# A Perceiver kernel on one core: the second block's convolution, running means and perceptron in four parts with a list of turns, its routing behind the second and the fourth part

## The chip, the cores and the metric

The kernel runs on one core of a Trainium2 chip. The core has a matrix engine (TensorE, "PE" in the profile, with its weight loads as "PEld"), VectorE (DVE), ScalarE (ACT), GpSimd (POOL), and a queue that issues transfers (SyncE, SP). Each works through its own instructions in a fixed order and waits for the others through semaphores. The metric is the time of one execution on the device in microseconds (us), smaller is better. All data is float32; in the trace one matrix product of this type is two records of PE, each with its weight load, and a transpose is one.

## The reference, cut to what matters

The network has four blocks, each of cross-attention, a sequence layer and a feed-forward layer, over x of 16 sequences by 64 steps by 256 features. The change touches the sequence layer and the routing of the second block (L1):

```python
x = x + L1_xattn(layernorm(x), ctx, ...)
x = x + L1_attn(layernorm(x), ...)
x = x + L1_ffn(layernorm(x), ...)

def L1_attn(x, ...):
    h = ln(x, ln_conv_g, ln_conv_b)
    x = x + causal_conv(h, conv_w, width=4, groups=4) + conv_b
    h = ln(x, ln_attn_g, ln_attn_b)
    q, k, v = h @ Wq.T + bq, h @ Wk.T + bk, h @ Wv.T + bv
    pooled_q = cumsum(q, axis=1) / arange(1, S + 1)
    pooled_k = cumsum(pooled_q * k, axis=1) / arange(1, S + 1)
    x = x + pooled_k * v
    h = ln(x, ln_boom_g, ln_boom_b)
    return x + gelu(h @ Wb.T + bb) @ Wu.T + bu

def L1_ffn(x, ...):
    probs = softmax(x @ router_W + router_b)
    top1 = argmax(probs)
    gates = one_hot(top1, 8) * probs
    h = relu(x @ W1[e] + b1[e])
    y = h @ W2[e] + b2[e]
    return sum over experts e of gates[e] * y
```

Wb makes 1024 features of 256, Wu 256 of 1024; the experts have 256, 1024 and 256.

## The kernel before

The 1024 rows of x (16 sequences of 64 steps) stay in on-chip memory as eight tiles of 128 rows, `xs`. The layers run one after the other (`run`, the `plan` table); each opens its own pools of on-chip memory and of the eight PSUM banks. Weights come through a ring of two slots: `pack()` waits for a layer's loads, which were issued earlier, and starts the next ones as soon as a slot is free.

`L1_attn` works through the layer in stages, each over all 1024 rows. `norm_x` (L184) normalizes the eight tiles, two transposes each. `norm` with `put_padded` does it again, with the affine part on VectorE (L1487), into `hp`, in which each sequence has three zero columns ahead. The convolution is products of 512 columns over shifted views of `hp`; ScalarE adds the bias (L1502). `add_by_features` transposes the outcome back and adds it (L1514). A third norm writes `hT` (L1521). Then, in four pieces (halves of the rows, halves of the features), q, k and v are products of 512 columns; `running_mean` is a sum along the steps on VectorE (L1540) and a product (L1541), k and v enter from PSUM (L1555, L1557). A second `add_by_features`, a fourth norm, and the perceptron, in two halves of 512 rows: eight products up with Gelu on ScalarE (L1572), then for each of four tiles eight products down, one of the bias row, and the addition to x (L89).

A norm of a tile (`norm_tile`, L150 to L161) is statistics on VectorE (L154, L156, L158), a power on POOL (L160), and a subtraction and product on VectorE (L170).

`L1_ffn` begins with `norm_x`, sends the rows to device memory (`keep_row`, L1082), makes the logits of eight tiles, and `route` (L1084 to L1143) finds each row's expert, its place among that expert's rows, and a table from place to row. `blocks` (L1237 to L1285) counts how many blocks of 128 rows each expert needs and lists the weight rows and token rows of each block. Then b2, weighted with the gate, is added to x for each tile: a transpose of the gates (L1360), a copy, a product, an addition. A block gathers its weights (`wa`, `wb`) and its rows (`hb`) by POOL's indirect transfers (L1304), transposes the rows (L179), and makes its products `ph` and `po`; 14 blocks run here.

Inside `L1_attn` and `L1_ffn` the order of instructions on each engine comes from a scheduler, which goes by priorities and a cost table when the kernel is built. Where `manual_schedule` names an engine, that engine keeps the order of the program text, as TensorE does in the cross-attention before.

## Time and profile before

| | |
|---|---|
| median of three runs | 3025.43 us (3025.0 to 3040.91) |
| the profiled execution | 3029.32 us, span of its instructions 3027.5 us |
| granted TensorE clock, mean | 0.942 |
| PE, PEld | 2704.1 us (89%), 1955.0 us (65%) |
| DVE, ACT, POOL | 1482.0 us (49%), 1022.6 us (34%), 309.4 us (10%) |
| transfers | 253.55 MB, mean 84 GB/s |

Busy time is the sum of an engine's instructions; a busy PE need not be PE at its peak, since ends of products are modelled and the clock changes. The granted clock is a share of full speed. In the timeline each line has a start, a duration, the engine, the line of the program, the operation, "output<-inputs", the shape and a count; what ended the idle time before it stands in brackets. The chain that ended last is followed back from the last instruction through what released each step. Many matrix products have the line of the helper `mm` (L69), so they are told apart by the names of their tiles.

### The profile page before, as it was taken

What the parts mean: (1) busy time and instruction counts of PE and PEld (TensorE: products, weight loads), DVE (VectorE), ACT (ScalarE), POOL (GpSimd) and SP (SyncE); (2) the same over time, 40 slices, a digit from 0 to 9 for tenths busy, and PEclk for the clock granted to TensorE, in tenths of its full rate; (3) what the DMA queues carried; (4) which work ended last, traced back from release to release, by engine and by line L of the source; (5) the groups of instructions that cost most, each with busy time, mean ns of one, the idle gap of its engine ahead of it and who ended that gap; (6) DMA issues with size and microseconds to landing.
All of it is one profiled execution on the core that took longest, in us unless ns stands there. A gap on an engine that the chain in (4) does not pass through costs nothing.

```text
span 3027.5 us, 42618 instructions
## 1 busy us (share of the span) xinstructions
PE 2704.1 (89%) x16840; PEld 1955.0 (65%) x16840; DVE 1482.0 (49%) x3177; ACT 1022.6 (34%) x2290; POOL 309.4 (10%) x428
## 2 busy tenths in 40 slices
PE   7888997999999787979999997887998898887899
PEld 3566784666666346857777776874766666665668
DVE  3654115666666643234444344223445657658581
ACT  2331122555555111223333321122335455455330
POOL 1112223000000112310101011201001000000000
PEclk9997997999999897989999998998999999998999
DMA  9504771101010004811111113450212212121110
GB/s 242 171 27 159 253 230 51 36 26 36 26 36 22 28 9 171 281 49 54 55 44 47 60 42 116 163 217 22 67 43 84 74 51 83 56 67 53 57 36 7
DMA packets 79220, 253.55 MB, mean 84 GB/s; under 512 B 15151, under 2 KB 26954, under 8 KB 69290
## 3 DMA queue, kind: packets, MB, share of 16 engines
q1 hardware_dynamic: 59562, 165.01, 17.5%
q0 software_dynamic: 13312, 80.28, 7.8%
q10 hardware_dynamic: 6144, 5.51, 0.5%
q8 instruction: 134, 2.20, 0.3%
q14 instruction: 68, 0.56, 0.1%
HBM read 233.80 MB, written 14.82 MB: 82 GB/s over the span
## 4 chain that ended last, share of the span: by engine, by line
PE 64%; DVE 11%; ACT 4%; DMA 3%; issue 3%; POOL 1%; SPq 1%; ACTq 0%; DVEq 0%; POOLq 0%
PE misc L69 11%; PE sc L500 8%; PE halves L69 7%; PE gu L69 5%; PE misc L235 4%; PE ps_h L69 4%; PE po L69 4%; PE ps_t L235 3%; PE sc L69 2%; PE misc L864 2%; ACT p L225 2%; PE o L915 2%; PE misc L878 2%; DMA back<-ys,route_at 2%; DVE x L1926 2%
## 5 line engine op out<-in xcount | busy, mean ns | idle before, releaser
L223 DVE TENSOR_REDUCE nmx<-sc 128x1 f32<-128x1024 f32 x264 | 311.6, 1218 | 234.9 <-PE sc L500 150.4
L225 ACT ACTIVATE p<-sc,nmx 128x1024 f32<-128x1024 f32 x264 | 294.6, 1116 | 312.1 <-DVE nmx L223 311.4
L500 PE MATMUL sc<-ctxT,qp 128*128 128x512 f32 (+1 forms) x1024 | 353.4, 599 | 0.0
L500 PEld LDWEIGHTS sc<-ctxT,qp 128*128 128x128 f32 (+1 forms) x1024 | 137.8, 189 | 153.0 <-issue 151.6
L69 PE MATMUL halves<-ctx,pT 128*128 128x192 f32 x1024 | 191.0, 343 | 9.4 <-DVE xs L89 4.0
L69 PEld LDWEIGHTS halves<-ctx,pT 128*128 128x128 f32 x1024 | 178.4, 203 | 12.3 <-DVE xs L89 4.5
L160 POOL TENSOR_TENSOR ln_rs<-ln_ve,nhalf 128x1 f32<-128x1 f32 x120 | 67.0, 563 | 1142.3 <-DVE ln_ve L158 1081.6
L69 PE MATMUL misc<-ctx,pT 128*128 128x192 f32 x1024 | 177.6, 327 | 0.5 <-DVE qT L465 0.5
L69 PEld LDWEIGHTS misc<-ctx,pT 128*128 128x128 f32 x1024 | 166.3, 191 | 2.1 <-DVE qT L465 1.0
L235 PE MATMUL ps_t<-ident,p 128*128 128x128 f32 x1088 | 147.2, 277 | 21.9 <-ACT p L225 14.0
L1916 ACT ACTIVATE da<-rep,al 128x252 f32<-128x252 f32 x256 | 114.7, 498 | 115.0 <-DVE x L1926 95.6
L1926 DVE TENSOR_TENSOR_SCAN x<-da,x 128x512 f32<-128x512 f32 x128 | 151.9, 1210 | 1.9 <-ACT da L1916 1.4
L235 PE MATMUL misc<-ident,p 128*128 128x128 f32 x1024 | 139.8, 283 | 14.1 <-ACT p L225 6.7
L237 ACT COPY pT<-ps_t 128x512 f32<-128x512 f32 x182 | 104.3, 585 | 139.3 <-PE ps_t L235 137.3
L235 PEld LDWEIGHTS ps_t<-ident,p 128*128 128x128 f32 x1088 | 127.1, 143 | 36.0 <-ACT p L225 17.7
L235 PEld LDWEIGHTS misc<-ident,p 128*128 128x128 f32 x1024 | 112.2, 143 | 40.2 <-ACT p L225 13.3
L69 PE MATMUL ps_h<-r,w 128*128 128x256 f32 x512 | 115.3, 385 | 0.0
L237 ACT COPY pT<-misc 128x512 f32<-128x512 f32 x128 | 75.0, 586 | 114.9 <-PE misc L235 114.6
L69 PEld LDWEIGHTS ps_h<-r,w 128*128 128x128 f32 x512 | 97.8, 192 | 16.6 <-issue 2.9
L69 PE MATMUL gu<-dT,wa 128*128 128x128 f32 (+1 forms) x864 | 104.7, 280 | 3.7 <-ACT dT L64 2.4
L239 DVE COPY pT<-misc 128x512 f32<-128x512 f32 x128 | 88.2, 689 | 39.4 <-PE misc L235 28.9
L69 PE MATMUL po<-wb,hid 128*128 128x256 f32 (+1 forms) x440 | 105.9, 388 | 0.2 <-ACT hid L1380 0.2
(468 smaller groups left out, 4449.5 us busy)
## 6 DMA issues: line engine op xcount, KB each, us to landing
ctx<-in_ctx SPq DMA_DIRECT2D x48, 768.0 KB
ctxT<-in_ctxT SPq DMA_DIRECT2D x48, 512.0 KB
w<-in_L2f_W SPq DMA_DIRECT2D x24, 1024.0 KB
rep<-dus SPq DMA_DIRECT2D x256, 64.0 KB
ctxT<-in_ctxT SPq DMA_DIRECT2D x16, 768.0 KB
ctxT<-in_ctxT SPq DMA_DIRECT2D x96, 128.0 KB
ys<-yb ACTq DMA_DIRECT2D x40, 128.0 KB
bc_rep<-bcs SPq DMA_DIRECT2D x32, 128.0 KB
```

What stands on the lines that cost most here:

```text
L69: self.nc.tensor.matmul(out, lhsT, rhs, start=n == 0, stop=n == len(pairs) - 1)
L160: nc.gpsimd.tensor_tensor(rs, ve, self.nhalf, ALU.pow)
L223: self.nc.vector.tensor_reduce(nmx, sc, AX.X, ALU.max, negate=True)
L225: self.nc.scalar.activation(p, sc, AF.Exp, bias=nmx, accum_out=sums)
L235: self.nc.tensor.transpose(ps[:, u, :], p[:, at : at + 128], self.ident)
L237: self.nc.scalar.copy(pT[:, 4 * g : 4 * g + 4, :], ps)
L239: self.nc.vector.tensor_copy(pT[:, 0:4, :], ps)
L500: nc.tensor.matmul(sc[u][:, bass.ts(kh, 512)], qp[n][par][rows, h : h + 2, :].rearrange("p h q -> p (h q)"), ctx[0][rows, at], start=n == ...
L864: nc.tensor.matmul(ps[kh], wk[:, kh, cols], cT[:, bass.ts(kh, 512)], start=True, stop=False)
L878: nc.tensor.matmul(ps[kh][:, u, :], cT[:, 512 * kh + at : 512 * kh + at + 128], wv[:, 0, :], start=u == 0, stop=False,)
L1916: nc.scalar.activation(da[:, g, :, 1:], now[j][:, 0, :].rearrange("p (b s) -> p b s", s=S)[:, :, 1:], AF.Exp, scale=al[:, col : col + 1],)
L1926: nc.vector.tensor_tensor_scan(flat, da.rearrange("p g b s -> p (g b s)"), flat, 0.0, ALU.mult, ALU.add)
```

## The change

`L1_attn` is written anew as a generator `part(p)` for 256 rows (two tiles), which yields at 15 places, and a generator `routing(first)` for four tiles, with five. `turns` lists which generator goes on next: 0, 1, 3, 4 are the four parts, 2 and 5 the routing of the first and of the last four tiles. TensorE keeps this order; the other engines are ordered by the scheduler as before.

Within a part, two tiles are normalized together, with one power for both; the affine part of the norms moves to ScalarE, as do the biases of k and v; four transposes share one PSUM bank; products have 256 columns; both halves of the features go through one sum of 512 columns. The layer closes its other PSUM pool and has eight one-bank buffers. The perceptron's outcome is normalized, sent to device memory and transposed by the part itself. `routing` holds the logits, `route`, and the addition of b2, all for four tiles; `L1_ffn` is left with `blocks` and the blocks. The router's weights and b2 are loaded with the perceptron's, so there is one pack less; the loads of the next block are started behind the turns.

```diff
     def gate(self, name, n=NT):
-        return (self.sb or self.lp).tile([128, n, E], F32, name=name)
+        return (self.sb or self.lp).tile([128, n, E], F32, bufs=self.gate_bufs, name=name)
...
-    def keep_row(self, i):
-
-        self.nc.sync.dma_start(self.hs[1 + i * 128 : 1 + (i + 1) * 128], self.htok[:, i, :])
+    def keep_row(self, i, x=None):
+
+        self.nc.sync.dma_start(self.hs[1 + i * 128 : 1 + (i + 1) * 128], self.htok[:, i, :] if x is None else x)
...
-    def pack_L1_gate(self):
-        self.slot()
-        w, row = self.load("L1f_rW"), self.load_row("L1f_rb")
-        b2 = self.carve(E, D)
-        self.nc.sync.dma_start(b2, self.a["L1f_b2"])
-        return w, row, b2
-
...
     def L1_ffn(self):
         nc = self.nc
-        rw, rb, b2 = self.pack()
-        self.norm_x()
-        self.routed = r = self.route_setup(1)
-        for i in range(NT):
-            self.keep_row(i)
-        gates = self.gate("gates")
-        for _ in self.route(r, self.gate_logits(rw, rb), 0, gates):
-            pass
-        self.rows, self.tokens = self.blocks(r, L1_BLOCKS)
-        for i in range(NT):
-            pg = self.misc([E, 128])
-            nc.tensor.transpose(pg, gates[:, i, :], self.ident)
-            gT = self.lp.tile([E, 128], F32, tag="gT", bufs=2, name="gT")
-            self.evict(gT, pg)
-            po = self.misc([128, D])
-            self.mm(po, [(gT, b2)])
-            self.add_to_x(i, po)
+        self.rows, self.tokens = self.blocks(self.routed, L1_BLOCKS)
+
         def block(j, own=""):
...
     def pack_L1_boom(self):
         self.slot()
-        return self.load("L1a_WbT"), self.load("L1a_WuT"), self.load_row("L1a_bu")
+        boom = self.load("L1a_WbT"), self.load("L1a_WuT"), self.load_row("L1a_bu")
+        gate = self.load("L1f_rW"), self.load_row("L1f_rb")
+        b2 = self.carve(E, D)
+        self.nc.sync.dma_start(b2, self.a["L1f_b2"])
+        return boom, gate, b2
 
     def L1_attn(self):
...
+        (cv, *qkv), ((wb, wu, bu), (rw, rb), b2) = self.pack(), self.pack(ahead=False)
+        self.lps_close()
+        routed, self.gate_bufs = self.route_setup(1), 4
+        later = self.later_steps()
+        def tokens(p, name):
+            return self.lp.tile([128, 2, D], F32, name=f"{name}{p}")
+        def features(p, name):
+            return self.lp.tile([128, 2, CHUNK], F32, name=f"{name}{p}")
+        def normalized(x, out):
+            mv = self.small.tile([128, 2, 2], F32, name="ln_mv2")
+            for t in range(2):
+                st = self.small.tile([128, 6], F32, name="ln_st")
+                nc.vector.bn_stats(st, x[:, t, :])
+                nc.vector.bn_aggr(mv[:, t, :], st)
+            rs = self.small.tile([128, 2], F32, name="ln_rs2")
+            nc.vector.tensor_scalar(rs, mv[:, :, 1], 1e-5, None, ALU.add)
+            nc.gpsimd.tensor_tensor(rs, rs, self.nhalf.to_broadcast([128, 2]), ALU.pow)
+            for t in range(2):
+                nc.vector.tensor_scalar(
+                    out[:, t, :], x[:, t, :], mv[:, t, 0:1], rs[:, t : t + 1], ALU.subtract, ALU.mult
+                )
+        def transposed(x):
+            ps = self.misc([128, 2, CHUNK])
+            for t in range(2):
+                for c in range(2):
+                    nc.tensor.transpose(ps[:, c, bass.ts(t, 128)], x[:, t, c * 128 : (c + 1) * 128], self.ident)
+            return ps
+        def affine(x, to, g, b):
+            ps = transposed(x)
+            for c in range(2):
+                src = ps[:, c, :]
+                if len(to.shape) == 4:
+                    src = src.rearrange("p (b s) -> p b s", s=S)
+                nc.scalar.activation(
+                    to[:, c], src, AF.Identity, bias=self.col(b, c), scale=self.col(g, c)
+                )
+        def added(x, to):
+            ps = self.misc([128, 2, D])
+            for t in range(2):
+                for c in range(2):
+                    nc.tensor.transpose(ps[:, t, bass.ts(c, 128)], x[:, c, t * 128 : (t + 1) * 128], self.ident)
+            nc.vector.tensor_tensor(to, to, ps, ALU.add)
+        by_features = [None] * NC
+        def part(p):
+            x = self.xs[:, 2 * p : 2 * p + 2, :]
+            hp = self.lp.tile([128, 2, 4, S + 3], F32, name=f"hp{p}")
+            nc.gpsimd.memset(hp[:, :, :, 0:3], 0.0)
+            x1, w = tokens(p, "x1"), tokens(p, "lnw")
+            normalized(x, x1)
+            normalized(x1, w)
+            yield
+            affine(w, hp[:, :, :, 3:], "L1a_lcg", "L1a_lcb")
+            yield
+            ps = self.misc([128, 2, CHUNK])
+            conv = features(p, "hTs")
+            for c in range(2):
+                self.mm(
+                    ps[:, c, :].rearrange("p (b s) -> p b s", s=S),
+                    [(cv[:, c, k, :], hp[:, c, :, k : k + S]) for k in range(4)],
+                )
+            for c in range(2):
+                nc.scalar.activation(conv[:, c, :], ps[:, c, :], AF.Identity, bias=self.col("L1a_conv_b", c))
+            yield
+            added(conv, x1)
+            w = tokens(p, "lnw")
+            normalized(x1, w)
+            yield
+            hT = features(p, "hTs")
+            affine(w, hT, "L1a_lag", "L1a_lab")
+            yield
+            got = []
+            for m, name in zip(qkv, "qkv"):
+                ps = self.misc([128, 2, CHUNK])
+                got.append(features(p, name))
+                for o in range(2):
+                    self.mm(ps[:, o, :], [(m[:, c, o * 128 : (o + 1) * 128], hT[:, c, :]) for c in range(2)])
+                for o in range(2):
+                    nc.scalar.activation(
+                        got[-1][:, o, :], ps[:, o, :], AF.Identity, bias=self.col(f"L1a_b{name}", o)
+                    )
+                if name == "q":
+                    yield
+            q, k, v = got
+            inv = self.inv_s.unsqueeze(1).to_broadcast([128, 8, S])
+            for y in (k, v):
+                flat = q.rearrange("p c t -> p (c t)")
+                nc.vector.tensor_tensor_scan(flat, later, flat, 0.0, ALU.mult, ALU.add)
+                steps = q.rearrange("p c (b s) -> p (c b) s", s=S)
+                nc.vector.tensor_tensor(steps, steps, inv, ALU.mult)
+                nc.vector.tensor_tensor(q, q, y, ALU.mult)
+            yield
+            added(q, x1)
+            w = tokens(p, "lnw")
+            normalized(x1, w)
+            nc.gpsimd.tensor_tensor(x, x, x1, ALU.add)
+            yield
+            hT = features(p, "hTs")
+            affine(w, hT, "L1a_lbg", "L1a_lbb")
+            yield
+            if p < 2:
+                g = self.act.tile([128, 8, CHUNK], F32, tag=("htok", "hT")[p], name="hid")
+            else:
+                g = self.lp.tile([128, 8, CHUNK], F32, name=f"hid{p}")
+            for m2 in range(4):
+                ps = self.misc([128, 2, CHUNK])
+                for u in range(2):
+                    m = 2 * m2 + u
+                    self.mm(ps[:, u, :], [(wb[:, c, m * 128 : (m + 1) * 128], hT[:, c, :]) for c in range(2)])
+                for u in range(2):
+                    m = 2 * m2 + u
+                    nc.scalar.activation(g[:, m, :], ps[:, u, :], AF.Gelu, bias=self.col("L1a_bb", m))
+                if m2 % 2:
+                    yield
+            for t in range(2):
+                po = self.misc([128, D])
+                self.mm(
+                    po,
+                    [(g[:, m, t * 128 : (t + 1) * 128], wu[:, m, :]) for m in range(8)] + [(self.ones[:1, :], bu)],
+                )
+                self.add_to_x(2 * p + t, po)
+                yield
+            o = tokens(p, "x1")
+            normalized(x, o)
+            for t in range(2):
+                self.keep_row(2 * p + t, o[:, t, :])
+            yield
+            by_features[p] = features(p, "hTs")
+            nc.scalar.copy(by_features[p], transposed(o))
+            yield
+        def routing(first):
+            ps = self.misc([128, 4, E])
+            for t in range(4):
+                hT = by_features[(first + t) // 2]
+                self.mm(
+                    ps[:, t, :],
+                    [(hT[:, c, bass.ts(t % 2, 128)], rw[:, c, :]) for c in range(2)] + [(self.ones[:1, :], rb)],
+                )
+            gates = self.gate(f"gates{first}", 4)
+            for _ in self.route(routed, ps, first, gates):
+                yield
+            yield
+            gTs = []
+            for t in range(4):
+                pg = self.misc([E, 128])
+                nc.tensor.transpose(pg, gates[:, t, :], self.ident)
+                gTs.append(self.lp.tile([E, 128], F32, tag="gT", bufs=4, name="gT"))
+                self.evict(gTs[t], pg)
+            yield
+            for t in range(4):
+                po = self.misc([128, D])
+                self.mm(po, [(gTs[t], b2)])
+                self.add_to_x(first + t, po)
+            yield
+        turns = "0010130134013004314101340301301403101341041134031434234323424242455555"
+        with self.tc.manual_schedule(engines={mybir.EngineType.PE}):
+            parts = [part(0), part(1), routing(0), part(2), part(3), routing(4)]
+            for p in turns:
+                next(parts[int(p)])
+        self.start_pack(self.at)
+        self.routed, self.gate_bufs = routed, 1
...
-            "L1_ffn": (self.L1_ffn, [self.pack_L1_gate]),
+            "L1_ffn": (self.L1_ffn, []),
...
-                    name=f"psm_{name}", bufs=3 if name == "L1_xattn" else 2, space=PSUM, reuse_waits="tile"
+                    name=f"psm_{name}", bufs={"L1_xattn": 3, "L1_attn": 8}.get(name, 2), space=PSUM, reuse_waits="tile"
```

## The prediction

> **What bounds the kernel now.** I looked first at the page's share of each engine (PE 89% busy, so idle or slow TensorE time is what can be won), then at the table of windows over the second block, the chain that ended last, and the timeline where one stage gives way to the next. Windows (the third number is TensorE busy time; the last three are granted clock, DMA share, GB/s):
>
> ```profile
> core 0: us, PE busy (x) PEld busy (x) DVE busy (x) ACT busy (x) POOL busy (x), PEclk, DMA share, GB/s
> 980.00:1000.00 20.00, 14.63 (x173) 9.86 (x172) 11.57 (x20) 8.57 (x17) 0.20 (x1) 1.00 0.05 10
> 1000.00:1020.00 20.00, 13.74 (x40) 6.51 (x40) 13.46 (x53) 1.62 (x4) 4.95 (x9) 0.74 0.23 98
> ...
> 1060.00:1080.00 20.00, 9.55 (x33) 4.27 (x31) 16.68 (x43) 1.97 (x2) 8.10 (x13) 0.74 0.01 1
> 1100.00:1120.00 20.00, 20.00 (x72) 13.00 (x72) 6.39 (x20) 2.06 (x3) 2.20 (x4) 1.00 0.08 26
> ...
> 284.00:288.00 4.00, 3.78 (x19) 3.06 (x17) 1.37 (x5) 0.38 (x1) 3.09 (x4) 1.00 1.04 433
> 998.40:1144.40 146.00, 121.38 (x384) 65.81 (x384) 77.76 (x230) 19.27 (x29) 23.24 (x41) 0.89 0.06 22
> 1144.40:1190.50 46.10, 31.75 (x115) 21.21 (x114) 19.32 (x89) 4.42 (x11) 9.11 (x10) 0.58 0.50 180
> 1190.50:1301.50 111.00, 106.72 (x698) 97.46 (x698) 22.61 (x63) 27.07 (x75) 31.14 (x33) 0.98 0.76 250
> ```
>
> From 998.4 (cross-attention's last addition to x) to 1144.4 (the last perceptron product) lies the stage that is rewritten: 146 us. From there to 1190.5 (first product of the first expert block) lie normalization, routing, and the gated b2: 46.1 us at half clock. The 14 blocks after it keep TensorE 96% busy; they just start earlier or later. In the first stretch TensorE is fully busy only in the perceptron; around 1010 and 1070 VectorE is the busy one and the clock falls to 0.74. The chain that ended last says the same: norms (DVE, POOL, PE in turn) and running sums release TensorE, until the perceptron, where it releases itself.
>
> ```profile
> 1037.84 0.56 POOL ln_rs L160
> 1038.42 0.42 DVE lnw L170
> ...
> 1064.77 1.24 DVE pk L1540
> ...
> 1096.69 16.90 PE misc L69 x72
> ```
>
> In the timeline (start, duration, engine, what) the second stretch ends in single file:
>
> ```profile
> 1100.70 3.72 PE L69 MATMUL misc<-w,hid 128*128 128x256 f32 x16
> 1104.35 0.69 PE L69 MATMUL misc<-w,ones 1*128 1x256 f32 x2
> ...
> 1166.82 0.60 PE L69 MATMUL misc<-route_seen,ones 128*128 128x8 f32 x2
> ...
> 1172.49 1.00 POOL L1304 DMA_INDIRECT wa<-in_L1f_W1b,rows  x1 [25.68 <-DVE first L1278]
> ...
> 1174.79 1.22 PE L69 MATMUL misc<-w,gT 8*128 8x256 f32 x2 [0.34 <-ACT gT L64]
> 1175.11 0.95 POOL L1304 DMA_INDIRECT hb<-hs,tokens  x1 [0.36 <-ACT gT L64]
> ...
> 1189.37 0.69 PE L179 MATMUL misc<-ident,hb 128*128 128x128 f32 x2
> ```
>
> The weight gather starts at 1172.5, yet the first block's transposes stand behind eight b2 products on TensorE, 1.9 us each, until 1189.4.
>
> **The change, first stretch.** TensorE's arithmetic stays, in pieces of 256 columns and in an order fixed by the turns, so its own work is the floor. A product is two records. Convolution 64, q/k/v 96 and perceptron up 128 make 288 records; a 256-column record in a full-clock stream costs 3.72/16 = 0.2325 us (a 512-column one is spaced 0.43, so halving costs some 8%): 67.0 us. Eight tiles of perceptron down are spaced 1104.97-1100.70 = 4.27 us: 34.2. Transposes come in fours; 24 groups, of which 23 stand ahead of the last perceptron product; four in a row took 0.66 us: 15.2. Routing of the first four tiles now stands inside: logits 0.86 us a tile at full clock (1149.63 to 1150.49), 3.4; ranks 0.7; table 8 records at 3.25/14, 1.9. Sum 122.4 us.
>
> To that come gaps, which I found by walking the built kernel's order of each engine with the durations of the rows. Nothing but part 0's first statistics is ready at 998.4: memset of "later" 0.48, normalization 0.82, second statistics 0.82, some of part 1's statistics queued between (0.9), power on POOL 0.85 with its waits, normalization 0.82: first transposes after 5.0 us. The first convolution waits 0.6 for ScalarE's affine and runs half cold: +2.7 (1.8 to 3.7). At about 18 us the next transposes of part 0 wait for VectorE, which has parts 1 and 2 queued ahead of them: 1.2; at about 43 those of part 0 after its running sums, behind part 1's first sum: 1.2. Hand-overs, 0.05 for each of 24 groups: 1. After that the walk finds each operand ready before its turn, as four parts stand between two stages of one part. 122.4 + 11.7 = 134 us against 146: **12 us saved**, with 128 to 146 as its bounds (no gap past the start; or every hand-over 0.5 us worse).
>
> Other engines do not become the bound. VectorE: 20 paired norms at 2.13 us, 8 additions from PSUM at 0.69, sums and products 8 x (1.22+0.69+0.69), 8 additions at 0.42: 72 us, and first routing some 10, of 134. ScalarE takes over affine and biases: 88 activations of 128x256, 0.474 us by the nearest rows with a bias tile, four copies at 0.59, two extra table loads at 1.28 (Exp in among Gelu; the trace has 1.28): 46 us. POOL: 20 powers at 0.55, four additions of 2 x 0.73. The additions stand ahead of a power in its queue, once at most 0.5 us late. On SP the three small router loads (0.3 us each) move behind the perceptron's weights, the next block's five loads follow the first two kept rows, and the "zero" rows wait behind a load for the slot of b2: nobody reads them before the next block. No wait for PSUM: eight banks go round. Norms of six tiles leave cross-attention, where VectorE had room: counted as 0, at most -3.
>
> [...] The new order has four places with three groups of transposes in a row, 2 us each. [...] The row at 980 to 1000 has a third of TensorE's work in transposes, and holes of 1.6 us, at 1.00. I take the row: 0[...].
>
> **Second stretch.** From the last perceptron product: addition and norm of two tiles 4.6 us (before 2.8 for one; VectorE's queue puts three b2 additions of the first half between), transposes 0.7, copy 0.65, logits of four tiles 5 (3.4 full, 5.9 half clock): 10.9, before 14.4. Softmax to route 2.85, ranks with three sums for seven 1.3, placing and four pairs of masks for eight 3.5, table 0.8, its addition 0.3: 19.6, before 26.2. Then, new on this path, four gate transposes and four b2 products *ahead* of the count of blocks (route_seen), which before stood amid the table: 0.8 + 3.8 + 0.6 = 5.2. Count to gather 2.2: first gather at 27.0 us, before 28.1. So that lead is spent; the gain is behind it, as no b2 product is left between gather and block. The block needs its 2.24 MB: at 433 GB/s (row 284) 5.2 us, with hb issued 2.6 us after[...]: 7.7; transposes and copy 1.3: 36 us against 46.1, **10 us saved**. Nothing before shows this landing alone: the lower end is 34.5; the upper is 44, if it takes the 16.9 us from 1172.5 to 1189.4. The first expert stage is nearest, 276.9 to 288.4, 11.5 us with TensorE held by other work; hence my 9. Blocks then take 8.1 us each against 5.2 of DMA, so the pace stays TensorE's.
>
> **Sum.** 12 + 10 = 22 us off the profiled span of 3027.5, whose execution took 3029.3. The median of the runs is 3025.43, so I forecast 3025.4 - 22 = **3003.3 us**.
>
> **Rivals.** (A) As worked, 2992 to 3010: chance 0.62. (B) Hand-overs between engines in a fixed order cost more: a turn whose operand is late holds up all parts. For: the gaps at 1003 to 1010, where TensorE waits 1.2 us per tile for a norm. Against: between two turns of one part there are 3 to 8 us of others'. With 0.4 us more at each of 33 turns, 13 us: 3016. Chance 0.17. (C) Landing, not b2, sets the first block: 44 in place of 36, 3011. For: DMA at 1.00 from 1176 to 1192. Against: that carries three blocks' sets. Chance 0.11. (D) The other side: the broken-up stream never holds full clock. The place is the rewritten stretch; the price is 122.4/c. At the 0.74 of the row 1000:1020, 165 + 12 = 177 us, 31 lost, 10 regained: 3046. It decides from c = 0.85 down (122.4/c = 146 + 10 - 11.7); for half a per cent slower c must be below 0.77. Against: that row is a quarter idle, the new stream should be over 90% busy. Chance 0.08. The remaining 0.02 is better than 2992. That the change doesn't do what it says is excluded by the built order.
>
> **Numbers.** Half a per cent, 15 us, is about what a measurement of this kernel can tell from no change: under 3010.3 is faster, over 3040.6 slower. Faster: A, the 0.02, a fifth of B and nearly half of C: 0.71. Slower: D less its milder half-clock forms, 0.07. Same: 0.22. Range 2991 to 3019: it leaves out D, the worse part of B, and the far end below.
>
> **What would show it.** Right: the last perceptron product some 134 us after cross-attention's last addition; clock near 1.00 from 15 us on; TensorE over 90% busy; first gather some 27 us after that product and the first block 9 after the gather. Wrong: holes in TensorE of 1 us or more at most turns, released by VectorE (B); hb landing later than 9 us (C); clock under 0.85 with TensorE queued full (D); or the blocks slower than 8.1 us each.

## The result and the profile after

The changed kernel took 3002.7 us, the median of five runs (3000.0 to 3004.5), where the kernel before, run beside it, took 3029.0 (3025.0 to 3040.9). The ratio is 0.9907 with a 95% interval of 0.9884 to 0.9929: about 28 us, nearly 1%, less. The forecast was 3003.3. Part of that nearness is luck: the three runs that the forecast started from, which are among the five of the comparison, had their median at 3025.4, some 3 us below that of the five, and the forecast took off 22 us where 26 to 28 came off.

The windows of the changed kernel's profile (columns as in the windows of before: TensorE busy time, weight loads, VectorE, ScalarE, GpSimd, then granted clock, DMA share, GB/s):

```profile
core 0 of [0], span 3002.8 us
core 0: us, PE busy (x) PEld busy (x) DVE busy (x) ACT busy (x) POOL busy (x), PEclk, DMA share, GB/s
1000.30:1015.00 14.70, 9.96 (x35) 7.61 (x36) 10.45 (x43) 2.77 (x6) 3.48 (x5) 0.76 0.39 145
1015.00:1128.20 113.20, 110.74 (x528) 92.83 (x527) 57.75 (x164) 40.93 (x89) 15.79 (x17) 0.95 0.08 26
1128.20:1163.60 35.40, 17.36 (x71) 13.17 (x71) 14.93 (x74) 3.45 (x8) 9.51 (x11) 0.58 0.35 117
1163.60:1273.70 110.10, 106.02 (x700) 97.18 (x700) 22.62 (x63) 27.04 (x75) 31.07 (x33) 0.98 0.82 272
```

The rows end at the landmarks of the forecast: cross-attention's last addition to x (1000.3), last perceptron product (1128.2), first product of the first expert block (1163.6), last product of the blocks (1273.7). From 1015 on TensorE is busy 98% of the time at 0.95, with VectorE at about half and ScalarE at a third. Below, the first and second stretch are the times between the first three landmarks, and the two together run from 1000.3 to 1163.6.

| us | before | forecast | after |
|---|---|---|---|
| first stretch | 146.0 | 134 | 127.9 |
| last perceptron product to first gather | 28.1 | 27.0 | 24.3 |
| first gather to first block | 18.0 | 9 | 11.05 |
| second stretch | 46.1 | 36 | 35.4 |
| the two together | 192.1 | 170 | 163.3 |
| blocks | 111.1 | 111 | 110.1 |

So 28.8 us were won where the change is, and one more in the blocks. The first stretch, at 127.9, came out just beyond the lower bound of 128 that the forecast gave it. Of the gain, 1.9 us are missing at the start, as x was ready at 1000.3 in place of 998.4: cross-attention's first attention products (`sc<-kT,qs`) start 2.9 us later than before, though nothing ahead of them was changed (in a second profile of the changed kernel 0.6 later), cross-attention is 2.3 us shorter up to its last ones, and the projection that ends it ran colder (1.99 us in the kernel before, at a granted clock of 1.00; 3.24 here, at 0.59). The last block product ends 27.9 us sooner. Another 3.1 go again in the next attention stage, which took 576.2 us before and 579.3 after though nothing in it was changed. Its first 20 us, before and then after:

```profile
1331.00:1341.00 10.00, 7.85 (x30) 3.87 (x30) 3.80 (x7) 4.95 (x8) 0.00 (x0) 0.93 0.00 0
1341.00:1351.00 10.00, 9.24 (x42) 5.56 (x40) 4.04 (x7) 3.23 (x6) 0.80 (x1) 1.00 0.26 79
```

```profile
1303.30:1313.30 10.00, 8.29 (x22) 3.42 (x21) 3.06 (x5) 3.74 (x6) 0.00 (x0) 0.78 0.00 0
1313.30:1323.30 10.00, 9.56 (x36) 5.35 (x35) 3.13 (x5) 2.11 (x5) 0.00 (x0) 0.83 0.15 52
```

The granted clock is 0.78 and 0.83 in place of 0.93 and 1.00, and 58 records are done there in place of 72. A second profile of the changed kernel (below) has 0.79 and 0.83 and 579.0 us; kernels that differ from it only in the second block had 574 to 579. As the stage itself is the same, what sets its clock lies outside it; which part of what runs before does so is open. That is why the experiments are read by the two stretches, and the run's time comes second.

TensorE in the changed kernel's timeline, first stretch (start, duration, engine, line, operation, output<-inputs, shape, count, and in brackets the idle time before it with what ended it):

```profile
1004.12 1.11 PE L1490 MATMUL misc<-ident,lnw 128*128 128x128 f32 x4 [4.36 <-DVE lnw L1481]
1005.99 6.05 PE L69 MATMUL misc<-hp,w 128*128 128x256 f32 x16 [0.75 <-ACT hp L1499]
...
1027.39 0.60 PE L1490 MATMUL misc<-ident,lnw 128*128 128x128 f32 x4
1027.83 0.60 PE L1508 MATMUL misc<-ident,hTs 128*128 128x128 f32 x4
1028.27 0.60 PE L1490 MATMUL misc<-ident,lnw 128*128 128x128 f32 x4
...
1041.51 1.09 PE L1490 MATMUL misc<-ident,lnw 128*128 128x128 f32 x4 [2.29 <-DVE lnw L1481]
1042.38 6.59 PE L69 MATMUL misc<-hTs,w 128*128 128x256 f32 x24
...
1106.48 0.59 PE L69 MATMUL misc<-w,ones 1*128 1x8 f32 x2
1107.00 6.75 PE L69 MATMUL misc<-w,hid 128*128 128x256 f32 x16
...
1118.70 3.62 PE L69 MATMUL misc<-w,hid 128*128 128x256 f32 x16
```

The reader sees the start (TensorE idle until 1004.1), the cold first convolution (granted clock 0.50 up to 1008.9), three groups of transposes spaced 0.44 us (1.00), one stall of 2.29 us and a slow spell behind it (0.50 from 1041.5 to 1044.5), and one perceptron product in 6.75 us where its like takes 3.62 (0.50 from 1107 to 1110). All other waits of the stretch are below 0.2 us. And the second stretch, with GpSimd's gathers of the first weights and of the tokens (`hb`) among TensorE's lines:

```profile
1144.46 1.97 PE L69 MATMUL misc<-s_col,s_who 128*64 128x128 f32 x8 [2.19 <-DVE s_col L1118]
1146.36 1.02 PE L1615 MATMUL misc<-ident,gates 128*8 128x128 f32 x4
1147.31 1.99 PE L69 MATMUL misc<-w,gT 8*128 8x256 f32 x8
1149.23 0.39 PE L69 MATMUL misc<-route_seen,ones 128*128 128x8 f32 x2
...
1152.55 1.02 POOL L1304 DMA_INDIRECT wa<-in_L1f_W1b,rows  x1 [21.01 <-DMA w<-in_L2a_BimT]
...
1155.12 0.95 POOL L1304 DMA_INDIRECT hb<-hs,tokens  x1 [0.30 <-issue]
...
1162.45 0.69 PE L179 MATMUL misc<-ident,hb 128*128 128x128 f32 x2 [8.95 <-DMA hb<-hs,tokens]
```

The gate transposes and b2 products stand ahead of the count (route_seen), as forecast; behind the gather, TensorE now stands idle for 8.95 us until the tokens land. The gather's bracket names a weight load, but a wait for it is not shown: with the count first (below), where these loads come later, the gather follows the count by the same 2.9 us.

### The profile page after: what moved, and what is told of

Its sections match the earlier page's. It is cut to its first block, busy times and chain, and to the rows that moved or that the text cites. A ratio compares the mean times of both kernels' runs of the same rounds, so it can differ in the third digit from the quotient of the medians.

```text
span 3002.8 us, 42857 instructions
## 1 busy us (share of the span) xinstructions
PE 2694.9 (90%) x16972; PEld 1985.8 (66%) x16972; DVE 1463.5 (49%) x3115; ACT 1045.4 (35%) x2353; POOL 302.4 (10%) x407
## 4 chain that ended last, share of the span: by engine, by line
PE 39%; DVE 9%; ACT 4%; DMA 3%; issue 3%; POOL 1%; SPq 1%; ACTq 0%; DVEq 0%; POOLq 0%
PE sc L500 8%; PE misc L69 8%; PE halves L69 7%; PE ps_h L69 4%; PE ps_t L235 3%; PE gu L69 2%; DVE x L1979 2%; PE po L69 2%; ACT p L225 2%; DMA back<-ys,route_at 2%; PE halves L2003 2%; DVE nmx L223 1%; DVE x L1975 1%; DVE x L1982 1%; PE large L69 1%
## 5 line engine op out<-in xcount | busy, mean ns | idle before, releaser
L223 DVE TENSOR_REDUCE nmx<-sc 128x1 f32<-128x1024 f32 x264 | 311.8, 1219 | 245.1 <-PE sc L500 153.3
L160 POOL TENSOR_TENSOR ln_rs<-ln_ve,nhalf 128x1 f32<-128x1 f32 x80 | 44.9, 567 | 733.2 <-DVE ln_ve L158 683.2
L69 PEld LDWEIGHTS gu<-dT,wa 128*128 128x128 f32 (+1 forms) x864 | 98.5, 185 | 10.9 <-ACT dT L64 4.8
## 6 DMA issues: line engine op xcount, KB each, us to landing
ctxT<-in_ctxT SPq DMA_DIRECT2D x96, 128.0 KB, 3.5
ys<-yb ACTq DMA_DIRECT2D x40, 128.0 KB, 4.8
bc_rep<-bcs SPq DMA_DIRECT2D x32, 128.0 KB, 3.2
```

The costliest lines, as they stand in the source:

```text
L69: self.nc.tensor.matmul(out, lhsT, rhs, start=n == 0, stop=n == len(pairs) - 1)
L160: nc.gpsimd.tensor_tensor(rs, ve, self.nhalf, ALU.pow)
L223: self.nc.vector.tensor_reduce(nmx, sc, AX.X, ALU.max, negate=True)
```

## The experiments

Theory T is the forecast's: the turns fill TensorE's waits with other parts' work; half of the routing and the b2 products leave the path to the first block. Against it stand the rivals of the forecast and others named with each run. The runs fall into three groups, beside which the kernel before took 3026.0 us (the three lists of turns and the affine on VectorE), 3032.7 (without b2, count first, logits sooner, first try) and 3028.3 (tokens first, all together, the changed kernel again), so a few us between run times of different groups say nothing.

### Is it the interleaving? Other lists of turns, same instructions

```diff
-        turns = "0010130134013004314101340301301403101341041134031434234323424242455555"
+        turns = "0" * 15 + "1" * 15 + "2" * 5 + "3" * 15 + "4" * 15 + "5" * 5
```

> The changed kernel with another list of turns: part 0 whole, part 1 whole, routing of the first four tiles whole, part 2, part 3, routing of the last four. Same pieces, same instructions, no interleaving. Theory T (the turns gain by filling TensorE's waits): between two stages of a part TensorE now waits for norms (about 4 us, three to four times a part), biases and affines (about 1 us, six times), running sums (about 5 us): some 25 to 29 us a part that nothing covers, so the first stretch takes 122 + 4 x 27 = about 230 us in place of 127.9, at a clock well under 0.9, and the run 3003 + 100 = about 3100 us or more. Rival R (the gain comes from fewer and cheaper instructions: paired norms, affines and biases on ScalarE, no routing of the first half behind the perceptron): the first stretch stays within 10 us of 127.9 and the run under 3015 us.

The first stretch took 235.9 us and the run 3104.4. Rival R, that fewer and cheaper instructions are the cause of the gain, is out: the same instructions one part after the other take 90 us more than the kernel before in that stretch (which there holds none of the routing). But the working of the expectation was wrong in two places that cancelled:

```profile
994.20:1230.00 235.80, 159.92 (x572) 122.26 (x572) 72.34 (x212) 45.46 (x97) 17.58 (x22) 0.75 0.06 22
```

TensorE is idle for 75.9 us, not 108; but it is busy for 159.9, not 122, at a clock of 0.75. So the gaps cost twice in this run: their own length, 68.7 us more than in the changed kernel, and 39.2 us more of busy time at the lower clock (0.75 in place of 0.93). (Busy time times clock is 119.9 us here and 112.3 in the changed kernel, so the mean clock accounts for most of the 39 us more of busy time, not all.)

```diff
-        turns = "0010130134013004314101340301301403101341041134031434234323424242455555"
+        turns = "0101010101010101010101010101013434343434342343423434234234234343455555"
```

> The changed kernel with turns that alternate part 0 with 1 to their ends, then part 2 with 3, routing of the first four tiles among the second pair as in the changed kernel, routing of the last four at the end. Only one other turn (0.6 to 4 us) now stands between two stages of a part. Theory T with the distance as the point: the chain of a part outside TensorE is about 27 us, one turn of the other part covers about a third to a half of it, so 14 to 18 us stay open for each pair; the first stretch takes 128 + 30 = about 158 us (150 to 170), the second stays at 35 to 38, the run is about 3033 us, no better than the kernel before. Rival T2 (two parts in flight are enough, since most waits are about as long as one turn): first stretch under 138, run under 3012 us.

```profile
1000.60:1180.40 179.80, 139.60 (x569) 112.40 (x570) 70.55 (x213) 44.60 (x96) 18.28 (x22) 0.82 0.08 28
```

The first stretch took 179.8 us (150 to 170 expected), the second 34.5, the run 3045.5, slower than the kernel before. T2 is out: two parts in flight are not enough. My figure for the idle time was fair (33 us more than in the changed kernel, 30 expected); what I left out is the clock again, 0.82, by which the same records take 18.9 us longer. In the first 50 us of this run TensorE waits six times for norms and running sums, 0.9 to 3.4 us at a time, behind the 4.36 us of the start. With four parts the waits are 7.2 us in all and the clock 0.93. The slow clock of rival D, in a broken stream, is seen here, with 40.2 us of waits.

### What is hiding half of the routing worth?

The order of the parts kept, the first four tiles' routing behind the last part:

```diff
-        turns = "0010130134013004314101340301301403101341041134031434234323424242455555"
+        turns = "0010130134013004314101340301301403101341041134031434343344442222255555"
```

> The changed kernel with the routing of the first four tiles moved behind the last part, just before that of the last four; the order of the parts themselves is kept. Theory T (hiding one half of the routing is worth what it takes in single file): the first stretch loses its TensorE work (logits 3.6, table 1.3, gate transposes and b2 on the far side, and the half-clock product behind the logits 3.1) and ends 6 to 9 us sooner, at 119 to 122; the second stretch gains logits, softmax, ranks, masks and table of four tiles, 12 to 18 us, and takes 47 to 54; the two together are 4 to 11 us longer than 163.3, the run 3007 to 3014 us. Rival (the routing of all tiles is one latency, and the first half rides along with the second): the two together within 2 us of 163.3.

```profile
997.60:1117.60 120.00, 112.74 (x524) 93.43 (x524) 62.40 (x173) 40.87 (x92) 19.30 (x22) 0.94 0.13 42
1117.60:1172.10 54.50, 29.79 (x107) 23.02 (x107) 21.90 (x108) 3.72 (x9) 9.47 (x11) 0.53 0.23 77
```

First stretch 119.9 (8.0 less), second 54.5 (19.1 more): 11.1 us net, at the far end of what T gave; the run took 3012.3. Of the 19.1 us more, TensorE is busy for 12.4 and idle for 6.7: over the whole stretch it is idle for 24.7 us, and its granted clock is 0.53. That is what routing in single file costs.

The first row also gives the change's first stretch without the routing, so it can be held against the 146 us of before: idle 7.2 in place of 24.6, busy 112.7 in place of 121.4. Busy time times clock is about the same, 106.0 against 108.0. So of the 26 us that the change won there, 17.4 are filled waits and nearly 9 are shorter busy time, which the clock, 0.94 in place of 0.89, accounts for; a cost of the pieces of half the width does not show.

### The affine on ScalarE

```diff
-                nc.scalar.activation(
-                    to[:, c], src, AF.Identity, bias=self.col(b, c), scale=self.col(g, c)
+                nc.vector.tensor_scalar(
+                    to[:, c], src, self.col(g, c), self.col(b, c), ALU.mult, ALU.add
                 )
```

> The changed kernel with the affine of the norms on VectorE (24 instructions of 128x256 from PSUM, as in the kernel before) in place of ScalarE. Theory T (neither engine bounds the stretch, TensorE does): VectorE goes from 68 to about 78 us of 125; the one place where TensorE waits for VectorE now (2.3 us) grows by one or two instructions, and a few others open; the first stretch takes 128 to 134 us, the run 3003 to 3009. Rival A (the gain rests on taking work off VectorE): all 10 us come back, first stretch 138 or more, run 3013 or more.

The first stretch took 132.2 us, in the range of T and 4.3 longer than in the changed kernel; the second 36.7; the run 3004.0. VectorE is busy for 79 of the 132 us, so it does not bound, but TensorE waits for it at each convolution:

```profile
1009.54 5.59 PE L69 MATMUL misc<-hp,w 128*128 128x256 f32 x16 [1.70 <-DVE hp L1499]
...
1017.85 3.69 PE L69 MATMUL misc<-hp,w 128*128 128x256 f32 x16 [1.25 <-DVE hp L1499]
...
1024.29 3.69 PE L69 MATMUL misc<-hp,w 128*128 128x256 f32 x16 [1.26 <-DVE hp L1499]
...
1035.95 3.69 PE L69 MATMUL misc<-hp,w 128*128 128x256 f32 x16 [1.48 <-DVE hp L1499]
```

In the changed kernel these waits are 0.75, none, none and 0.17 us. What ScalarE gives is a short queue for the first turns, where VectorE has four parts' norms to do; 5 to 6 of the 29 us rest on it. The paired norms, the biases on ScalarE and the eight PSUM buffers were not tried alone.

### What held the first block before?

The kernel before without its gated b2 (the loop of gate transposes, products and additions to x is left out, and so is that term of the output):

```diff
-        for i in range(NT):
-            pg = self.misc([E, 128])
-            nc.tensor.transpose(pg, gates[:, i, :], self.ident)
...
-            self.mm(po, [(gT, b2)])
-            self.add_to_x(i, po)
```

> The kernel before with the eight gated b2 products (gate transposes, products, additions to x) left out; the output lacks the b2 term. The question is what held the first expert block in the kernel before, 18.0 us behind its first gather. Theory T (TensorE's queue of b2 products did; the landing of the first set alone takes about 11 us, as in the changed kernel): the first gather stays at 28 us behind the last perceptron product, the first block's product follows it by 10 to 12 us, so it starts 6 to 8 us sooner than before. Rival C (the landing of weights and rows held it): the first block's product stays within 2 us of 46.1 us behind the last perceptron product, and TensorE idles there instead.

```profile
1173.48 1.00 POOL L1304 DMA_INDIRECT wa<-in_L1f_W1b,rows  x1 [25.68 <-DVE first L1278]
...
1183.28 0.69 PE L179 MATMUL misc<-ident,hb 128*128 128x128 f32 x2 [8.15 <-DMA hb<-hs,tokens]
1184.42 5.79 PE L69 MATMUL ph<-dT,wa 128*128 128x128 f32 x26 [0.46 <-ACT dT L64]
```

The gather stands where it stood (28.1 us behind the last perceptron product) and the first block follows it by 10.9 us in place of 18.0: 7.1 us were TensorE's queue of b2 products, the rest is landing. (The run took 3019.9 us, once, some 13 less than the kernel before beside it; what goes beyond the 7.1 lies outside this stretch.) Rival C, that the landing set the block before, is out; but the landing is right behind, and it is longer than the 9 us that I took.

### What stands ahead of the gather, and what is in the landing?

The last four tiles' gate transposes and b2 products behind the count (their gates are kept in a spare third of the routing's tile):

```diff
-        turns = "0010130134013004314101340301301403101341041134031434234323424242455555"
+        turns = "00101301340130043141013403013014031013410411340314342343234242424555"
...
+        self.rest = parts[5]
...
         self.rows, self.tokens = self.blocks(self.routed, L1_BLOCKS)
+        for _ in self.rest:
+            pass
```

> The changed kernel with the gate transposes and b2 products of the last four tiles moved behind the count of blocks and its table look-up; the next block's weight loads and the zero rows move behind the first gather with them. Theory G (the forecast's 5.2 us step: what stands ahead of the count on TensorE delays the gather by its length): first gather 2.5 to 4 us sooner, at 20 to 22 us behind the last perceptron product in place of 24.3; TensorE's wait for hb takes the b2 products in, and the first block starts 3 to 5 us sooner if the landing stays at 9 to 11 us. Run 2998 to 3000. Rival S (the landing, not the gather's start, is what ends last[...]): the gather moves but the first block does not, and the run stays within 1 us of 3002.7.

```profile
1140.69 0.60 PE L69 MATMUL misc<-route_seen,ones 128*128 128x8 f32 x2
...
1144.20 1.02 POOL L1304 DMA_INDIRECT wa<-in_L1f_W1b,rows  x1 [18.23 <-issue]
...
1146.78 0.95 POOL L1304 DMA_INDIRECT hb<-hs,tokens  x1 [0.30 <-issue]
...
1145.15 1.46 PE L1617 MATMUL misc<-ident,route 128*8 128x128 f32 x4
1146.59 3.80 PE L69 MATMUL misc<-w,gT 8*128 8x256 f32 x8
1154.49 0.66 PE L179 MATMUL misc<-ident,hb 128*128 128x128 f32 x2 [4.10 <-DMA hb<-hs,tokens]
```

The gather comes at 21.5 us behind the last perceptron product, 2.8 sooner, and the first block at 32.9, 2.5 sooner than in the changed kernel. The gather moved as theory G said; the block gained a little less than its 3 to 5. The b2 products (5.3 us) now lie wholly in TensorE's wait for the tokens, which was 8.95 us and is 4.10. The run took 2996.1 us, below the 2998 to 3000 expected; its ratio to the kernel before is 0.9883 (0.9867 to 0.99), which overlaps that of the changed kernel.

The second half of the question: the changed kernel, but each block gathers its tokens ahead of its second weights.

```diff
         self.gather_rows(w, self.a["L1f_W1b"], self.rows[:, j : j + 1])
+        dT = self.block_tokens(j, own)
         w2 = self.lp.tile([128, 8 * D], F32, tag="wb" + own, bufs=1 if own else 3, name="wb")
...
-            dT = self.block_tokens(j, own)
```

> The changed kernel with one order changed: each expert block gathers its first weights (wa), then its tokens (hb), then its second weights (wb); before and after it was wa, wb, hb. The first block's transposes need hb alone, its first product hb and wa. Theory Q (the 11 us from the first gather to the first block are a queue of transfers: hb stands behind 2.1 MB of weights, all of which must land ahead of it): hb now stands behind half of them, so TensorE's wait for it shrinks and the first block starts 7 to 9 us behind the first gather, 2 to 4 us sooner. Rival L (the 11 us are a fixed latency of a gather with what runs beside it, whatever is ahead): it stays at 10.5 to 11.5 us.

```profile
1151.30 1.02 POOL L1304 DMA_INDIRECT wa<-in_L1f_W1b,rows  x1 [21.01 <-DMA w<-in_L2a_BimT]
1152.74 0.95 POOL L1304 DMA_INDIRECT hb<-hs,tokens  x1 [0.42 <-issue]
...
1159.30 0.69 PE L179 MATMUL misc<-ident,hb 128*128 128x128 f32 x2 [7.04 <-DMA hb<-hs,tokens]
1160.45 4.76 PE L69 MATMUL ph<-dT,wa 128*128 128x128 f32 x29 [0.46 <-ACT dT L64]
```

The first block follows the gather by 9.15 us in place of 11.05 (11.54 in the second profile of the changed kernel), just short of the 2 to 4 us expected of theory Q. The rest of that kernel is as it was (first stretch 128.0, gather at 24.3). So L, 11 us whatever stands ahead, doesn't fit. But the 1.9 us are not all a queue of transfers: GpSimd issues the tokens 1.44 us behind the first gather here and 2.57 in the changed kernel, which is 1.1 of them. From their own issue to TensorE's transposes the tokens took 6.56 us, in place of 7.33 and 7.82 in the two profiles of the changed kernel; 0.8 to 1.3 us, at most, are left for a queue. The run took 2993.0 us, once, where the changed kernel beside it took 2999.9; most of that difference lies outside the two stretches.

### Why did one product take 6.75 us?

The logits of the first four tiles one turn sooner:

```diff
-        turns = "0010130134013004314101340301301403101341041134031434234323424242455555"
+        turns = "0010130134013004314101340301301403101341041134031432434323424242455555"
```

> The changed kernel with one swap in the list of turns: the logits of the first four tiles one turn sooner, ahead of part 3's first four perceptron groups in place of behind them. What is tested is why one perceptron product ran in 6.75 us in place of 3.6 in the changed kernel. Theory K (the thin logits products, 8 columns each, make the clock fall to half[...]): the 16 products of part 3's perceptron up behind the logits now take 6.3 to 7 us, and the perceptron-down product that was slow takes 3.6 to 3.8. Rival M (that product was slow for itself: its weights, or a transfer beside it): it stays near 6.75 us wherever the logits stand. The run's time stays the same, 3003.

```profile
1100.84 0.59 PE L69 MATMUL misc<-w,ones 1*128 1x8 f32 x2
1101.36 5.13 PE L69 MATMUL misc<-hTs,w 128*128 128x256 f32 x16
1106.32 3.62 PE L69 MATMUL misc<-w,hid 128*128 128x256 f32 x16
```

The slow spell went with the logits: the product that was slow takes 3.62 us again, and the perceptron up behind the logits is slow. Rival M is out. It was slow for a shorter time (5.13 us against the 6.3 expected, 1.4 to 1.6 us lost in place of 3.1). The first stretch is 126.4, the run 2999.0. The logits are 3.5 us of products with 8 columns without a gap, and the last one is slow already (0.59 us where its like took 0.38): the slow spell began here with no idle time ahead of it. In the changed kernel the granted clock is 1.00 from 1101 to 1103, ahead of the logits, and 0.50 from 1107 to 1110, behind them. How much of the next product is slow varies: 6.75 and 6.77 us in two profiles of the changed kernel, 6.75 with the tokens first, 5.41 with the affine on VectorE, 5.13 here; with the count first, seven of its records took 3.17 us where their like took 1.68.

### Put together, and the changed kernel again

A first try: the count first, all b2 products behind the gather, the logits spread over four turns of the perceptron, and part 2's q product ahead of part 0's last affine, for which TensorE waited 2.29 us.

```diff
                     [(hT[:, c, bass.ts(t % 2, 128)], rw[:, c, :]) for c in range(2)] + [(self.ones[:1, :], rb)],
                 )
+                if first == 0 and t < 3:
+                    yield
...
-        turns = "0010130134013004314101340301301403101341041134031434234323424242455555"
+        turns = "001013013401300431410134301030140310134104113403142324232432342444555"
...
+        self.rest = parts[2], parts[5]
```

> As the one with the count first, with the b2 of the first four tiles behind the count too, the logits of the first four tiles spread one tile at a time between turns of the perceptron, and part 2's q product moved ahead of the affine that TensorE waited 2.3 us for. Theory T: the spread logits leave the clock full (3 us less), the swap closes the hole (1 to 2.3 us less), b2 of the first four leaves the wait before the last part's transposes and VectorE's queue there (0 to 2 us less), the count first 3 to 5 us: 7 to 12 us less than the changed kernel, 2991 to 2996. Rival (each hole closed opens another as long): not under 2999.

The run took 2995.7 us (ratio 0.9883, 0.9866 to 0.9899), in the range, but no better than the count alone. The two stretches took 157.7 us, 5.6 less than in the changed kernel, below the 7 expected. First stretch 124.2: no product behind the logits is slow any more (all perceptron products 3.62 to 3.72), but the hole of 2.29 us became two, of 0.51 and 1.36. And all eight b2 products (3.8 us for four; the clock of the second stretch is 0.54) with their transposes now fill the landing to its end: the first block stands 12.6 us behind the gather, behind b2 once more.

So the next one keeps the first four tiles' b2 where it was, in the wait ahead of the last part's transposes, and takes the tokens ahead of the second weights:

```diff
-        turns = "001013013401300431410134301030140310134104113403142324232432342444555"
+        turns = "00101301340130043141013430103014031013410411340314232423243234242424555"
...
-        self.rest = parts[2], parts[5]
+        self.rest = parts[5:]
...
+        dT = self.block_tokens(j, own)
         w2 = self.lp.tile([128, 8 * D], F32, tag="wb" + own, bufs=1 if own else 3, name="wb")
```

> The changed kernel with four things together: the count of blocks ahead of the last four tiles' gate transposes and b2; the logits of the first four tiles spread over turns of the perceptron; part 2's q product ahead of the affine of part 0; tokens gathered ahead of the second weights. The b2 of the first four tiles stays in the wait ahead of the last part's transposes. From the single runs: first stretch 124 us (127.9 in the changed kernel), first gather at 21 to 22 us (24.3), first block 8 to 11 us behind it (11.05; the b2 products of 5.3 us lie inside). If the parts add up the two stretches take 153 to 157 us in place of 163.3, and the run is 2990 to 2996 us. Rival (parts hide one another, since b2 now stands between gather and block): 158 us or more, no better than the one with the count first.

```profile
1142.85 1.02 POOL L1304 DMA_INDIRECT wa<-in_L1f_W1b,rows  x1 [18.35 <-DVE at_block L1270]
1144.83 0.95 POOL L1304 DMA_INDIRECT hb<-hs,tokens  x1 [0.95 <-PE misc L1620]
...
1145.23 3.80 PE L69 MATMUL misc<-w,gT 8*128 8x256 f32 x8
1149.07 0.66 PE L179 MATMUL misc<-ident,hb 128*128 128x128 f32 x2
1150.25 5.75 PE L69 MATMUL ph<-dT,wa 128*128 128x128 f32 x32 [0.52 <-ACT dT L64]
```

TensorE goes from the last b2 product to the block without a wait: the tokens landed within 6.2 us of the gather, and the block stands 7.4 us behind it. First stretch 124.3, second 29.1, together 153.3 before rounding: the parts add up.

> The changed kernel itself, unaltered, beside the others. What is asked is how far the stretches and the time of one kernel vary from execution to execution: the two stretches within 1.5 us of 163.3, the time from cross-attention's last addition backwards and from the last expert block onwards free to vary by 3 to 4 us each, the run 3000 to 3005 us.

In these runs the changed kernel took 2999.9 us (2996.7 to 3002.9) and the version with all four 2991.1 (2988.2 to 2995.8), against 3028.3 of the kernel before: ratios 0.9908 (0.9891 to 0.9924) and 0.9879 (0.986 to 0.9898). It is 9 us below the changed kernel, with no run of the one within the range of the other. Whether it is faster than the count alone or the first try, whose ratios were 0.9883 in another group of runs, is not shown by the run times; its two stretches are shorter (153.3 in place of 159.3 and 157.7). The second profile of the changed kernel has 128.0 and 35.9 us in its two stretches, 163.9 in place of 163.3; x was ready 2.5 us sooner than in the first. So the stretches repeat within a microsecond, and what lies around them does not. The median is slightly below the 3000 to 3005 expected.

## Why the prediction was right, step by step

**First stretch, 12 us forecast, 18.1 measured.** The mechanism is right (the three runs with other lists of turns). Of the sum, these terms were mis-sized:

| term, us | forecast | measured |
|---|---|---|
| start until the first transposes | 5.0 (its items add up to 4.7) | 3.8 |
| 288 records of 256 columns | 67.0 | 62.9 (16 in 3.45 to 3.56, from start to start) |
| 23 groups of transposes | 15.2 | 10.1 (0.44 each in the stream) |
| routing of the first four tiles | 6.0 | 4.9 (logits 3.56, ranks 0.36, table 1.02) |
| cold first convolution | 2.7 | 2.4 (5.88 less 3.45, from start to start; clock 0.50 up to 1008.9) |
| stalls at 18 and 43 us | 1.2 + 1.2 | none, 2.3 |
| half clock behind the stall (0.50 from 1041.5 to 1044.5) | 0 | 1.7 (0.43 on the transposes, 1.26 on 24 records) |
| half clock behind the logits (0.50 from 1107 to 1110) | 0 | 3.1 |
| hand-overs (0.05 each, an estimate of mine) | 1 | under 0.5 |

The largest error, 9 us, is one of reading: I divided the length of a group in the timeline by its records (3.72/16; 0.66 for four), but a group's length runs to the end of its last record, while the next group starts before that (0.60 us from 1027.39, and the next at 1027.83). Measured from start to start, a record of 256 columns takes 0.216 to 0.222 us, and one with 512 takes 0.43: halving cost 3% at most here, where I had put 8%. The clock took 4.8 us back, at two places that I had put at nothing. With the perceptron down as forecast (34.2) and 0.75 for the first convolution's wait, the measured terms come within 1.5 us of the stretch; 0.9 of these are two more slow groups of transposes near the start (1.11 us long at a granted clock of 0.50, and 0.91 at 1.00).

**The transposes.** For the places with three groups in a row I put 0, by the row at 1.00. That stands: the three groups at 1027.39 are spaced 0.44 us at a granted clock of 1.00, not the 0.87 that the group at 1041.51 takes at 0.50, and the window from 1015 on is at 0.95. The slow spells from there on stand elsewhere: behind the stall of 2.29 us (1.7 us lost) and behind the thin logits (3.1).

**Second stretch, 10 us forecast, 10.7 measured.** Logits done at 10.3 (10.9 forecast), the table's products at 18.2 (19.6 with their addition, which ends at 18.5 here), gate transposes, b2 and count 3.2 (5.2; the four b2 products took 1.9 us here, and 3.7 in the count-first run), count to gather 2.9 (2.2). The gather stands at 24.3 in place of 27.0. The landing then took 11.05 in place of 9. Two errors of 2 to 3 us cancelled, which is luck. The forecast's landing was an estimate: 5.2 us for 2.24 MB at the 433 GB/s of one row, the tokens' issue 2.6 us behind (7.7 as written), and 1.3. In the changed kernel's trace the tokens are issued 2.57 us behind the gather, take 7.33 to TensorE's transposes, and the block follows 1.15 later, together 11.05. So the term that was too small is the landing itself, 5.2 in place of 7.33. That the lead of the half routing is partly spent by putting b2 ahead of the count was right (2.8 us of the gather, by the run with the count first). That before the block hung on b2 was right too (7.1 us, by the run without b2).

**Other engines** do not bound, as forecast: VectorE 68.2 us of 127.9 (82 forecast), ScalarE 43.7 (46). I put the norms leaving cross-attention at 0 with -3 as the bound; from its first attention product to the start of its last, cross-attention is 2.3 us shorter (498.7 in place of 501.0), but what follows up to the last addition to x is 1.3 longer, with the colder projection.

**The rivals.** B (0.4 us more at each hand-over): apart from the one stall and the first convolution's wait no wait is over 0.2 us. C (the landing, not b2): 35.4, not 44; its landing is real, but the shorter of the two. D (the stream never at full clock): 0.95 from 15 us on; the runs with other lists of turns show what D looks like, 0.75 and 0.82. The total, 22 us forecast at the first block, was 28.8 there, and 24.7 of these are left at the end of the profile; that the losses outside the two stretches bring the total nearer to the forecast is luck.

## What to carry to other kernels

When parts of a chain are interleaved in a fixed order, count the parts in flight: here two left 40 us of waits and four left 7. With the 33 us more of waits came 18.9 us more of busy time, at a clock of 0.82 in place of 0.93; with one part at a time, 68.7 and 39.2 us, at 0.75. Measure the pace of a stream from start to start of its groups, not by a group's length. After a stage is moved, look at what is now next on the path: here it was the order of three gathers and of two small products, which, with the spread logits and the earlier q product, were worth 10 us more in the two stretches, a third of the change's own gain.

## What the runs showed that I had not expected

- Products of 8 columns without a gap for 3.5 us were followed by a slow spell in six profiles, which cost the next product 1.5 to 3.1 us; the same products spread one tile at a time between others (0.8 us each) were not (3.62 to 3.72 us for the next). Why the slow part varies between profiles is not shown by any run here.
- With repeated waits, of up to 3.94 us in the first 36 us of one run and 4.36 in the first 50 of the other, the clock was 0.75 and 0.82 on the mean over 236 and 180 us.
- The landing of the tokens was shorter where less was issued ahead of them. Counted from their own issue, the tokens took 7.2 to 7.8 us behind both weights (7.33 and 7.82 in the changed kernel, 7.71 with the count first, 7.19 in the kernel before without b2), 6.56 behind the first weights alone, and at most 4.24 in the last kernel. The next block's weight loads were issued just ahead of the gather in the changed kernel (1149.3 to 1152.3, as b2's slot comes free) and with the tokens first, but not in the other three; behind both weights no cost of them shows. What makes the last step, from 6.56 to 4.24, wasn't tried alone.
- The third block's attention starts at 0.78 and 0.79 in the two profiles of the changed kernel, where nothing in it was changed, and that took 3 of the 28 us away again. What sets it I have not found.
